# GpSimd makes the query-key products of a windowed attention, in halves of 1024 elements, and the schedule of the expert walk is paced for it

## The chip, the core and the metric

The kernel runs on one core of a Trainium2 chip. Its engines are called as in the profile: PE (TensorE, matrix products; PEld its weight loads), DVE (VectorE), ACT (ScalarE), POOL (GpSimd) and SP, which here only issues transfers. Each engine takes its own list of instructions in order and waits on semaphores for the others. The metric is the device time of one execution in microseconds (us).

## The reference

The input x is (2, 1024, 256) in float32. It is normalised over the last axis (xn), and the output is x plus an attention branch of xn plus a mixture-of-experts branch of xn.

The attention branch sees each batch as 64 × 64 × 4 = 16384 tokens of 16 channels. Two branches of 8 channels attend inside windows of 8 neighbouring tokens, one along rows and one along columns. Cut to what matters:

```python
qkv = (tok @ qkv_w).reshape(B, -1, 3, C)
attn = softmax(part(q) * scale @ swapaxes(part(k), -1, -2), axis=-1)
out = attn @ vw + lepe                       # lepe: a 3x3 depthwise convolution of v
att = concatenate([x1, x2], axis=-1) @ proj_w + proj_b
normed = (att - mu) * rsqrt(var + EPS) * ln_w + ln_b
return transpose(tok + normed, (0, 2, 1)).reshape(B, H, W)
```

The other branch routes each of the 2048 rows to 6 of 16 experts of 176 hidden units (silu(x Wg) * (x Wu), then Wd), weighted, and adds two shared experts.

## The kernel before

A prologue normalises x, computes the routing, sorts the rows by their sets of experts into 16 tiles of 128 rows, and does the shared experts. Then comes **the walk**, which this change concerns.

The walk goes over **slots**. A slot is one visit of one expert to one sorted tile: 16 tiles × 6 slots, and 26 slots called extras for tiles that need more experts, done after the first four tiles; 122 in all, and a loop for rare leftovers. Slots come in pairs (units) with a software pipeline over the unit u:

- `up` (L831 to L834), once a slot: PE multiplies the tile with the expert's gate and up weights into PSUM (pr_u, three buffers), ACT makes the silu (sg), and DVE multiplies sg, the routing weight and the up half into `hms`. There are two buffers of hms, each for one unit.
- `hidden` (L845, L847), once a unit, for unit u-1: PE transposes hms (ph), ACT copies it (hT).
- `finished`, once a unit, for unit u-2: PE multiplies with the down weights (pr_y, L857 for pairs, L865 for extras). DVE or ACT adds it to ysum (L912 for pairs, L920 for extras).
- `added`: when a tile's sum is complete, POOL scatters it into the output with an indirect DMA (L926). These accumulate into the same output, so each waits for the one before to land.

Between the slots the walk places the **steps of the attention**: after the preparation of weights, four blocks (batch b, head h), then eight steps `attended` (L750 on) that project, normalise and collect the attention's rows in `att`, and adds to the output (L954, POOL's queue).

A block has these steps. `project` (L660 to L665), eight times: PE makes q, k and v of an eighth of the block's tokens, ACT copies them into qk and v. Then four times, for 4 of 16 window groups (NW = 4): `products` (L673), DVE multiplies each query with each key element by element into a buffer of 2048 elements a partition, and `scores` (L677), DVE sums over the 8 channels. Then `highest` (L683 to L685): maximum, subtraction, and the exponential on ACT. Then four times `weighted` (L694) and `values` (L699), DVE's product of weights with values and its sum, and between them `totals` (L688, L689). Then `divide` (L707), and `transposed` (L714, L716): PE's transposes po and ACT's copy to oT. products and weighted use the same buffer (tag prod, one buffer).

The order of the work is decided twice. In the program, each step carries a pair of costs in us for DVE and PE, and a slot has such a pair too (`of_slot`). After every slot the walk emits steps as long as DVE's summed cost is no larger than `pace` times PE's:

```python
while step and done[0] <= pace * done[1]:
    step[2]()
    counted(step)
    last, step = step, next(walk, None)
    if last[1] > 1:
        break
```

`pace` is the ratio of the whole walk's DVE cost to its PE cost, both without the last END us of PE. Then the framework's scheduler orders the instructions of each engine by its own estimate of when they can start; the lists of the engines are fixed before the kernel runs.

Of the kernel before, what the change touches and what calls it, by code (L numbers as in the profile page):

```python
# [8 lines left out]
F32 = mybir.dt.float32  # L9
# [4 lines left out]
ALU = mybir.AluOpType  # L14
AX = mybir.AxisListType
# [7 lines left out]
P = 128  # L23
B, H, W = 2, 1024, 256
C = 16
HD = 8
WIN = 8
NW = 4
# [21 lines left out]
def csw_block_moe(ctx: ExitStack, tc: tile.TileContext, x, qkv_w, conv_w0, conv_b0, conv_w1, conv_b1,  # L50
# [19 lines left out]
    nc = tc.nc  # L70
# [3 lines left out]
    work = ctx.enter_context(tc.tile_pool(name="work", bufs=1))  # L74
# [8 lines left out]
    def by_hl(t):  # L83
        return t.rearrange("(p l) d -> p l d", l=16)
# [3 lines left out]
    for g in range(4):  # L88
        (nc.sync if g % 2 == 0 else nc.scalar).dma_start(out=xx[:, 4 * g : 4 * g + 4, 0:W],
                                                         in_=by_hl(x_rows)[:, 4 * g : 4 * g + 4, :])  # L90
# [41 lines left out]
    for b in range(B):  # L132
        nc.gpsimd.dma_start(out=lb[64 * b : 64 * b + 64, :],
                            in_=ln_b.rearrange("(c o) -> c o", o=1).unsqueeze(1).to_broadcast([C, 4, 1]))
# [14 lines left out]
    for c in range(16):  # L149
        n = sum(P // 2 if k % 2 == 0 else P for k in range(c)) + (((16 - c) * P - 1) / 2 if c % 2 == 0 else 0)  # L150
# [69 lines left out]
    def statistics(g):  # L220
        st = small.tile([P, 4, 6], F32, name="st")
        mv = small.tile([P, 4, 2], F32, name="mv")
        for l in range(4):
            nc.vector.bn_stats(out=st[:, l, :], in_=xx[:, 4 * g + l, 0:W])
        for l in range(4):
            nc.vector.bn_aggr(out=mv[:, l, :], in_=st[:, l, :])
        rs = small.tile([P, 4], F32, name="rs")
        nc.scalar.activation(rs, mv[:, :, 1], AF.Sqrt, bias=eps)
        return mv, rs
# [88 lines left out]
    held = statistics(0)  # L318
    for g in range(4):
        now, held = held, statistics(g + 1) if g < 3 else None  # L320
# [15 lines left out]
    full = [P, 16, E]  # L336
# [114 lines left out]
    for c in range(15, -1, -1):  # L451
        n = 16 - c
# [186 lines left out]

    oT = big.tile([P, 4, 2, 4, P], F32, name="oT", tag="oT")  # L640

    def attention(b, h):
        steps = []

        qk = work.tile([P, 2, 2, 8, WIN, HD], F32, tag="qk", name=f"qk{b}{h}")
        v = work.tile([P, 2, 8, HD, WIN], F32, tag="v", name=f"v{b}{h}")
        s = work.tile([P, 16, WIN, WIN], F32, tag="f1024", name=f"s{b}{h}", bufs=3)
        o = work.tile([P, 16, WIN, HD], F32, tag="f1024", name=f"o{b}{h}", bufs=3)
        sums = small.tile([P, 16, WIN], F32, name=f"sums{b}{h}", tag="sums")
        rows = work.tile([P, 8, P], F32, tag="f1024", name=f"rows{b}{h}", bufs=3)  # L650
        full = [P, NW, WIN, WIN, HD]

        def gather():
            for i in range(2):
                nc.scalar.copy(rows[:, 4 * i : 4 * i + 4].rearrange("p i (w r) -> p i w r", r=4),
                               xnT[:, h, :, 64 * b : 64 * b + 64].rearrange("p (i r) (w u) -> p u i w r", r=4, u=2)[:, i])

        def project(i):
            pq = ps_m.tile([P, 3, 8, C], F32, tag="m", name="pq")
            nc.tensor.matmul(pq.rearrange("p s t c -> p (s t c)"), lhsT=rows[:, i],  # L660
                             rhs=wq.rearrange("p s t c -> p (s t c)"), start=True, stop=True)
            nc.scalar.copy(qk[:, :, 0, i], pq[:, 0:2, :, 0:HD])  # L662
            nc.scalar.copy(qk[:, :, 1, :, i], pq[:, 0:2, :, HD:C])
            nc.scalar.copy(v[:, 0, i], pq[:, 2, :, 0:HD].rearrange("p t c -> p c t"))
            nc.scalar.copy(v[:, 1, :, :, i], pq[:, 2, :, HD:C])  # L665

        held = {}

        def products(n):
            pr = work.tile([P, NW, WIN, WIN, HD], F32, tag="prod", name="pr")  # L670
            br, m = n // 8, n % 8
            q_, k_ = (qk[:, part, br, m : m + NW] for part in range(2))
            nc.vector.tensor_tensor(pr, q_.unsqueeze(3).to_broadcast(full), k_.unsqueeze(2).to_broadcast(full), ALU.mult)  # L673
            held[n] = pr

        def scores(n):
            nc.vector.tensor_reduce(out=s[:, n : n + NW], in_=held.pop(n), axis=AX.X, op=ALU.add)  # L677

        rows_s = s.rearrange("p n q k -> p (n q) k")

        def highest():
            top = small.tile([P, P], F32, tag="top", name="top", bufs=1)
            nc.vector.tensor_reduce(out=top, in_=rows_s, axis=AX.X, op=ALU.max)  # L683
            nc.vector.tensor_tensor(rows_s, rows_s, top.unsqueeze(2).to_broadcast([P, P, WIN]), ALU.subtract)
            nc.scalar.activation(rows_s, rows_s, AF.Exp, scale=HD**-0.5)  # L685

        def totals():
            nc.vector.tensor_reduce(out=sums.rearrange("p n q -> p (n q)"), in_=rows_s, axis=AX.X, op=ALU.add)  # L688
            nc.vector.reciprocal(sums, sums)  # L689

        def weighted(n):
            pr = work.tile([P, NW, WIN, HD, WIN], F32, tag="prod", name="pv")
            br, m = n // 8, n % 8
            nc.vector.tensor_tensor(pr, s[:, n : n + NW].unsqueeze(3).to_broadcast(full),  # L694
                                    v[:, br, m : m + NW].unsqueeze(2).to_broadcast(full), ALU.mult)
            held[n] = pr

        def values(n):
            nc.vector.tensor_reduce(out=o[:, n : n + NW], in_=held.pop(n), axis=AX.X, op=ALU.add)  # L699

        def divide():
            xo = held["xo"] = work.tile([P, 8, 8, C], F32, tag="xo", name=f"xo{b}{h}")
            for br in range(2):
                to = xo[:, :, :, HD * br : HD * br + HD]
                if br:
                    to = to.rearrange("p i t c -> p t i c")
                nc.vector.tensor_tensor(to, o[:, 8 * br : 8 * br + 8],  # L707
                                        sums[:, 8 * br : 8 * br + 8, :].unsqueeze(3).to_broadcast([P, 8, WIN, HD]),
                                        ALU.mult)

        def transposed(i):
            po = ps_m.tile([P, 4, P], F32, tag="m", name="po")
            for j in range(4):
                nc.tensor.transpose(po[:, j, :], held["xo"][:, i + j].rearrange("p t c -> p (t c)"), ident)  # L714
            to = oT.rearrange("p g h r (b w i) -> p g h b i w r", b=B, i=2)[:, :, h, b, i // 4]
            nc.scalar.copy(to, po.rearrange("p j (w r) -> p j w r", r=4))  # L716


        steps.append((0.3, 0.0, gather))
        for i in range(8):  # L720
            steps.append((0.3, 0.65, lambda i=i: project(i)))
        for n in range(0, 16, NW):
            steps.append((2.3, 0.0, lambda n=n: products(n)))
            steps.append((2.3, 0.0, lambda n=n: scores(n)))
        steps.append((2.5, 0.0, highest))
        for n in range(0, 16, NW):
            steps.append((2.3, 0.0, lambda n=n: weighted(n)))
            if n == 0:
                steps.append((1.5, 0.0, totals))
            steps.append((2.3, 0.0, lambda n=n: values(n)))  # L730
        steps.append((1.4, 0.0, divide))
        for i in (0, 4):
            steps.append((0.3, 0.5, lambda i=i: transposed(i)))
        return steps
# [195 lines left out]
    att = []  # L930

    def all_steps():
        for steps in (extras_listed(), weights_prepared()):
            for _ in steps:
                yield 1.0, 0.1, lambda: None
        yield from attention_steps()

    def attention_steps():
        for b in range(B):
            for h in range(2):  # L940
                yield from attention(b, h)
        xe = []
        yield 0.6, 0.0, lambda: xe.extend(edges())
        att.extend(work.tile([P, 8, W], F32, tag=tag, name="att") for tag in ("prod", "qk"))
        for g in range(4):
            for h in range(2):
                yield 1.4, 3.9, lambda: attended(g, h, xe, att)
            if g % 2:
                waiting.extend([lambda m=m, b=b, n=g // 2: attention_added(m, b, n) for m in range(2) for b in range(B)])
# [7 lines left out]

    of_slot = {"six": (0.5, 2.0), "extra": (1.4, 2.25)}
    of_tile = (1.05, 0.25)
    END = 66  # L960
    in_walk = [11 * 1.0 + 4 * (16 * 2.3 + 3.3 + 2.5 + 1.5 + 1.4) + 0.6 + 8 * 1.4, 11 * 0.1 + 4 * 6.2 + 8 * 3.9]
    done = [0.0, 0.0]
    whole = [in_walk[n] + NTL * TOPK * of_slot["six"][n] + NX * of_slot["extra"][n] + NTL * of_tile[n] for n in range(2)]
    pace = (whole[0] - END * of_slot["six"][0] / of_slot["six"][1]) / (whole[1] - END)

# [121 lines left out]
```

## Time and profile before

| | |
|---|---|
| median of 7 runs (lowest to highest) | 466.79 us (464.4 to 470.0) |
| the profiled execution: time, span | 464.15 us, 462.4 us |
| granted TensorE clock, mean | 0.987 |
| PE, DVE, ACT, POOL busy | 412.6, 305.4, 214.2, 108.8 us |
| products L673 | 16 of 2289 ns, 36.6 us |
| scores L677 | 16 of 2280 ns, 36.5 us |
| weighted L694, values L699 | 16 of 2286 ns and 16 of 2268 ns |
| hms L834, pairs alone | 96 of 392 ns |
| scatters L926 on POOL | 16 of 1974 ns, 3.9 us to landing |

A timeline row of the profile has the start in us from the span's start, the duration in us, engine, line, operation, output and inputs, the shapes, how many instructions were merged into the row, and in brackets the idle time of the engine before it with what ended that. Rows of DVE overlap by some 0.08 us, so the distance from start to start is the better measure of what an instruction costs in a run of them. The chain of waits follows back from the last instruction what released it.

The walk runs in the profile from about 101 us (first slot) to 448 us. The four blocks' projections begin at 134.4, 196.3, 263.2 and 318.0 us, and the first attended step at 372.8 us.

### The profile page before, as it was taken

Reading aid. Unit: us, or ns where it says so; the run is one execution under the profiler, and the core shown is the slowest. Engines: PE = TensorE matmul, PEld = TensorE weight load, DVE = VectorE, ACT = ScalarE, POOL = GpSimd, SP = SyncE. Lnnn points to the kernel's source line nnn. Section 1 sums busy time; section 2 is a strip of 40 time slices with the busy share of each in tenths; the row PEclk is TensorE's granted clock in tenths of the full one; section 3 lists DMA queues with packets and bytes.
Section 4 is the critical chain, followed back from the end, with each engine's and each line's share of the span. In section 5 each row is a group of like instructions: output and inputs, shape, how many; then the busy total and the mean of one; then the engine's idle time right before and its main releaser. Section 6 shows DMA issues by size and latency. Waiting matters only on the chain.

```text
span 462.4 us, 6437 instructions
## 1 busy us (share of the span) xinstructions
PE 412.6 (89%) x1726; PEld 259.1 (56%) x1727; DVE 305.4 (66%) x555; ACT 214.2 (46%) x510; POOL 108.8 (24%) x127
## 2 busy tenths in 40 slices
PE   0999999996999998999999999998998889999980
PEld 0436566563666665655556666665666545556760
DVE  4525956745729999469999289995999932333220
ACT  2936167222354464463642453625343247778220
POOL 7300000426500000000001222110221126666821
PEclk9999999998999999999999999999999999999996
DMA  8999970423310010000001321201013110185552
GB/s 235 322 291 277 258 214 1 97 46 87 91 38 21 22 29 24 26 7 28 20 24 27 55 39 37 43 24 27 23 35 84 35 17 16 50 123 95 71 80 23
DMA packets 38323, 35.39 MB, mean 77 GB/s; under 512 B 4112, under 2 KB 36208, under 8 KB 38256
## 3 DMA queue, kind: packets, MB, share of 16 engines
q1 hardware_dynamic: 28336, 23.28, 18.3%
q0 software_dynamic: 8896, 10.65, 14.7%
q10 hardware_dynamic: 1056, 1.05, 0.7%
q8 instruction: 16, 0.26, 0.2%
q14 instruction: 19, 0.16, 0.1%
HBM read 26.44 MB, written 10.62 MB: 80 GB/s over the span
## 4 chain that ended last, share of the span: by engine, by line
PE 39%; DVE 35%; issue 9%; ACT 7%; DMA 6%; DVEq 1%; POOL 1%; POOLq 0%; SPq 0%; ACTq 0%
PE pr_u L831 10%; DVE pr L673 6%; PE pp L766 6%; DVE s L677 6%; DVE pv L694 5%; DVE o L699 5%; PE pr_y L857 5%; DVE hms L834 4%; PE pg L270 3%; DMA xg<-xw_d,of 3%; PE py L285 2%; PE pq L660 2%; PE pu L270 2%; DMA xx<-in_x_dram 2%; PE plT L252 2%
## 5 line engine op out<-in xcount | busy, mean ns | idle before, releaser
L831 PE MATMUL pr_u<-w1s,xsT 128*128 x384 | 127.8, 464 | 0.7 <-DVE hms L834 0.5
L833 ACT ACTIVATE sg<-pr_u 128x176 f32<-128x176 f32 x122 | 38.6, 318 | 134.5 <-PE pr_u L831 109.2
L831 PEld LDWEIGHTS pr_u<-w1s,xsT 128*128 128x128 f32 x384 | 71.6, 191 | 35.8 <-issue 5.5
L926 POOL DMA_INDIRECT out_dram<-ysum,of x16 | 31.6, 1974 | 225.2 <-ACT sg L833 124.5
L834 DVE SCALAR_TENSOR_TENSOR hms<-sg,w,pr_u 128x176 f32<-128x176 f32 x96 | 36.9, 392 | 35.3 <-ACT sg L833 35.3
L673 DVE TENSOR_TENSOR pr<-qk 128x2048 f32<-128x2048 f32 x16 | 36.6, 2289 | 20.0 <-ACT qk L662 19.7
L845 PE MATMUL ph<-ident,hms 128*128 128x128 f32 x183 | 33.8, 280 | 8.7 <-DVE hms L834 7.3
L845 PEld LDWEIGHTS ph<-ident,hms 128*128 128x128 f32 x183 | 23.4, 142 | 29.7 <-DVE hms L834 13.2
L694 DVE TENSOR_TENSOR pv<-s,v 128x2048 f32<-128x2048 f32 x16 | 36.6, 2286 | 2.4 <-ACT s L685 2.4
L677 DVE TENSOR_REDUCE s<-pr 128x256 f32<-128x2048 f32 x16 | 36.5, 2280 | 0.0
L699 DVE TENSOR_REDUCE o<-pv 128x256 f32<-128x2048 f32 x16 | 36.3, 2268 | 0.0
L831 PE MATMUL pr_u<-w1s,xd 128*128 x104 | 33.5, 460 | 0.0
L847 ACT COPY hT<-ph 128x384 f32<-128x384 f32 x61 | 29.1, 478 | 3.1 <-PE ph L845 1.5
L857 PE MATMUL pr_y<-w2a,hT 128*128 x96 | 28.7, 381 | 0.0
L857 PE MATMUL pr_y<-w2b,hT 112*128 x96 | 28.7, 379 | 0.0
L857 PE MATMUL pr_y<-wts,hT 128*128 128x256 f32 x96 | 28.6, 379 | 0.0
L660 PE MATMUL pq<-wq,rows 128*128 128x384 f32 x64 | 24.7, 502 | 2.8 <-ACT oT L716 2.1
L285 PE MATMUL py<-room 128*128 128x256 f32 x96 | 23.9, 387 | 1.5 <-DVE room L279 1.5
L831 PEld LDWEIGHTS pr_u<-w1s,xd 128*128 128x128 f32 x104 | 19.6, 190 | 9.3 <-issue 0.4
L270 PE MATMUL pg<-xnT,room 128*128 128x512 f32 x48 | 24.1, 614 | 0.0
L270 PE MATMUL pu<-xnT,room 128*128 128x512 f32 x48 | 23.0, 602 | 0.0
L285 PEld LDWEIGHTS py<-room 128*128 128x128 f32 x96 | 17.4, 190 | 6.8 <-DVE room L279 2.6
(320 smaller groups left out, 640.1 us busy)
## 6 DMA issues: line engine op xcount, KB each, us to landing
w1s<-in_w_dram SPq DMA_DIRECT2D x22, 256.0 KB, 5.5
wts<-in_w_dram SPq DMA_DIRECT2D x61, 64.0 KB, 2.1
wts<-in_w_dram SPq DMA_DIRECT2D x61, 48.0 KB, 1.8
xw_d<-xx SPq DMA_DIRECT2D x4, 544.0 KB, 8.9
w2a<-in_w_dram SPq DMA_DIRECT2D x4, 512.0 KB, 10.5
out_dram<-ysh POOLq DMA_DIRECT2D x4, 512.0 KB, 5.6
xr<-xw_d POOLq DMA_DIRECT2D x4, 512.0 KB, 5.0
out_dram<-att POOLq DMA_DIRECT2D x8, 256.0 KB, 6.7
```

Source lines behind the costliest of these rows:

```text
L270: nc.tensor.matmul(ps, lhsT=w1h[:, half, h, P * m : P * m + P], rhs=xnT[:, h, 4 * k : 4 * k + 4, :].rearrange("p l q -> p (l q)"), start=( ...
L285: nc.tensor.matmul(py, lhsT=hms[k, m][:, P * c : P * c + P], rhs=w2h[:, m], start=(m == 0), stop=(m == 2))
L660: nc.tensor.matmul(pq.rearrange("p s t c -> p (s t c)"), lhsT=rows[:, i], rhs=wq.rearrange("p s t c -> p (s t c)"), start=True, stop=True)
L673: nc.vector.tensor_tensor(pr, q_.unsqueeze(3).to_broadcast(full), k_.unsqueeze(2).to_broadcast(full), ALU.mult)
L677: nc.vector.tensor_reduce(out=s[:, n : n + NW], in_=held.pop(n), axis=AX.X, op=ALU.add)
L694: nc.vector.tensor_tensor(pr, s[:, n : n + NW].unsqueeze(3).to_broadcast(full), v[:, br, m : m + NW].unsqueeze(2).to_broadcast(full), ALU. ...
L699: nc.vector.tensor_reduce(out=o[:, n : n + NW], in_=held.pop(n), axis=AX.X, op=ALU.add)
L831: nc.tensor.matmul(pu, lhsT=lhs[:, h, :], rhs=w1s[:, :, h, bass.ds(e * I, I)], start=(h == 0), stop=(h == 1))
L833: nc.scalar.activation(sg, pu[:, 0, :], AF.Silu)
L834: nc.vector.scalar_tensor_tensor(hm[:, 0:I], sg, w, pu[:, 1, :], op0=ALU.mult, op1=ALU.mult)
L845: nc.tensor.transpose(ph[:, s, :], units[:, P * s : P * s + P], ident)
L857: nc.tensor.matmul(py, lhsT=l_, rhs=r_, start=start and n == 0, stop=stop and n == 2)
```

## The change

The products move from DVE to POOL (`nc.gpsimd.tensor_tensor`), in 8 chunks of 1024 elements a partition instead of 4 of 2048. One buffer `prods` of two halves is made once and kept for all blocks; the chunks alternate between the halves, and weighted uses both halves as one buffer of 2048. scores reduces a chunk of 1024 at a time. The steps are emitted one chunk apart (products of chunk n, then scores of chunk n-1), each with a DVE cost of 1.8 us instead of 2.3. The sum of costs `in_walk` and END (66 to 62) are changed to match, so `pace` becomes 1.33 instead of 1.18. The later buffer `att` takes the place of prods. In the changed file the lines are products L681, scores L685, maximum L691, weighted L702, values L707, hms L844, scatter L936.

```diff
+    prods_ = []
+
     def attention(b, h):
         steps = []
+        if not prods_:
+            prods_.append(work.tile([P, 2, NW // 2, WIN, WIN, HD], F32, tag="prod", name="prods"))
+        prods = prods_[0]
...
+        few = NW // 2
+        fewer = [P, few, WIN, WIN, HD]
+
         def products(n):
-            pr = work.tile([P, NW, WIN, WIN, HD], F32, tag="prod", name="pr")
+            pr = prods[:, n // few % 2]
             br, m = n // 8, n % 8
-            q_, k_ = (qk[:, part, br, m : m + NW] for part in range(2))
-            nc.vector.tensor_tensor(pr, q_.unsqueeze(3).to_broadcast(full), k_.unsqueeze(2).to_broadcast(full), ALU.mult)
+            q_, k_ = (qk[:, part, br, m : m + few] for part in range(2))
+            nc.gpsimd.tensor_tensor(pr, q_.unsqueeze(3).to_broadcast(fewer), k_.unsqueeze(2).to_broadcast(fewer), ALU.mult)
             held[n] = pr
 
         def scores(n):
-            nc.vector.tensor_reduce(out=s[:, n : n + NW], in_=held.pop(n), axis=AX.X, op=ALU.add)
+            nc.vector.tensor_reduce(out=s[:, n : n + few], in_=held.pop(n), axis=AX.X, op=ALU.add)
...
         def weighted(n):
-            pr = work.tile([P, NW, WIN, HD, WIN], F32, tag="prod", name="pv")
+            pr = prods.rearrange("p a w q k d -> p (a w) q k d")
...
-        for n in range(0, 16, NW):
-            steps.append((2.3, 0.0, lambda n=n: products(n)))
-            steps.append((2.3, 0.0, lambda n=n: scores(n)))
+        for n in range(0, 16 + few, few):
+            if n < 16:
+                steps.append((1.8, 0.0, lambda n=n: products(n)))
+            if n >= few:
+                steps.append((1.8, 0.0, lambda n=n: scores(n - few)))
...
-    END = 66
-    in_walk = [11 * 1.0 + 4 * (16 * 2.3 + 3.3 + 2.5 + 1.5 + 1.4) + 0.6 + 8 * 1.4, 11 * 0.1 + 4 * 6.2 + 8 * 3.9]
+    END = 62
+    in_walk = [11 * 1.0 + 4 * (16 * 1.8 + 8 * 2.3 + 3.3 + 2.5 + 1.5 + 1.4) + 0.6 + 8 * 1.4, 11 * 0.1 + 4 * 6.2 + 8 * 3.9]
```

More of the change, by code (lines that the diff above doesn't have):

```diff
@@ L943, in attention_steps @@
         yield 0.6, 0.0, lambda: xe.extend(edges())
-        att.extend(work.tile([P, 8, W], F32, tag=tag, name="att") for tag in ("prod", "qk"))
+        att.extend([prods_[0].rearrange("p a w q k d -> p (a w q k d)").rearrange("p (n d) -> p n d", d=W),
+                                       work.tile([P, 8, W], F32, tag="qk", name="att")])
         for g in range(4):
```

## The prediction, made before the changed kernel was run

> **What bounds the kernel now.** I read the page first: busy shares, slices, the chain.
>
> ```profile
> PE 412.6 (89%) x1726; PEld 259.1 (56%) x1727; DVE 305.4 (66%) x555; ACT 214.2 (46%) x510; POOL 108.8 (24%) x127
> ...
> DVE  4525956745729999469999289995999932333220
> ...
> POOL 7300000426500000000001222110221126666821
> ...
> PE 39%; DVE 35%; issue 9%; ACT 7%; DMA 6%; DVEq 1%; POOL 1%; POOLq 0%; SPq 0%; ACTq 0%
> ```
>
> PE (TensorE) is busy nearly everywhere, so a gain needs PE's waits to go. DVE (VectorE) is at nine tenths in four stretches, the four attention blocks (two batches, two heads), where POOL (GpSimd) is nearly idle. The chain runs through DVE there: L673, L677, L694, L699. Next, the timeline of DVE and of PE in the fourth block:
>
> ```profile
> 322.01 2.29 DVE L673 TENSOR_TENSOR pr<-qk 128x2048 f32<-128x2048 f32 x1 [5.57 <-ACT qk L662]
> 324.22 0.39 DVE L834 SCALAR_TENSOR_TENSOR hms<-sg,w,pr_u 128x176 f32<-128x176 f32 x1
> 324.53 2.28 DVE L677 TENSOR_REDUCE s<-pr 128x256 f32<-128x2048 f32 x1
> ...
> 342.59 1.22 DVE L683 TENSOR_REDUCE top<-s 128x128 f32<-128x1024 f32 x1
> ...
> 346.39 2.29 DVE L694 TENSOR_TENSOR pv<-s,v 128x2048 f32<-128x2048 f32 x1 [0.81 <-ACT s L685]
> ...
> 370.83 0.41 DVE L912 TENSOR_TENSOR ysum<-ysum,pr_y 128x256 f32<-128x256 f32 x1
> ```
>
> ```profile
> 317.99 1.81 PE L660 MATMUL pq<-wq,rows 128*128 128x384 f32 x4 [0.70 <-ACT oT L716]
> ...
> 336.49 2.53 PE L831 MATMUL pr_u<-w1s,xsT 128*128 x8
> 338.85 0.27 PE L845 MATMUL ph<-ident,hms 128*128 128x128 f32 x1
> 339.92 0.44 PE L845 MATMUL ph<-ident,hms 128*128 128x128 f32 x2 [0.80 <-DVE hms L834]
> ...
> 372.77 1.12 PE L766 MATMUL pp<-xnT,lp 128*128 128x512 f32 x2
> ```
>
> A block is a DVE chain: projection at 317.99, first product 4.0 later, products and scores to 342.6 (20.6), maximum to weights 3.8, values 24.4 to 370.8; the next PE stage starts 1.9 later. It lasts 54.8 us. Beside it PE does 20 to 22 slots of expert work. A slot has one hms on DVE; two slots are a unit of 4.0 us on PE (transposes L845 at 436.52 and 440.52 in the chain). PE waits for hms, 0.3 to 0.9 us at a time: it can run only two slots ahead, since the transposes (ph) after slot 2u+2 need the hms of slot 2u. All of PE's waits for DVE in the walk, by the waits view, are 7.3 (hms), 3.4 (ysum) and 1.7 (xo): 12.4 us. That is the largest gain that a lighter DVE could give.
>
> **What the change removes and adds.** DVE loses 16 products of 2.29 = 36.6 us. The 16 reductions of 2048 become 32 of 1024; the nearest row is the maximum over 1024 (L683, 1.22, its successor starting after 1.13): 32 × 1.2 = 38.4 against 36.5. DVE's net relief is some 35 us. POOL gets 32 products. Its nearest rows:
>
> ```profile
> 381.51 1.27 POOL L782 TENSOR_TENSOR a<-a,lw 128x512 f32<-128x512 f32 x1 [7.45 <-DVE a L781]
> 382.87 2.09 POOL L787 TENSOR_TENSOR att<-a,xr 128x256 f32<-128x256 f32 x2
> ```
>
> Two halves of 1.27 less one start (0.1, the smallest memset) make 2.44 for 1024 elements. Low end: the line through 256 elements in 1.05 and 512 in 1.27 gives 1.72. High end: four of L787's 1.05 are 4.2; that row reads with long strides, the products read runs of 8 contiguous floats with a broadcast, like L782's runs of 16. So I take 2.45 with the gap to the next.
>
> [...]
>
> What matters is that a chunk on POOL (2.45) costs as much as half a product and half a score on DVE (2.28): the chain through a score phase, 8 × 2.45 + 1.2 for the last reduction = 20.8, is no shorter than the 20.6 of now. POOL can't start early: prods is the buffer of the values too, and qk comes from PE and ACT. Two halves let POOL run back to back.
>
> **What the order does.** The built program lists each engine's instructions. DVE's list for the third block from the first product or score to the maximum (P product, S score, h hms, y ysum, T maximum):
>
> ```
> before  P h S P h S h P h S h y P h S h T
> after   S h S S S S S h S h S T
> ```
>
> Each S now waits for POOL, and the hms behind it wait with it. PE gets three hms in 20 us where it got seven, so it runs dry: the up products (L831) of two slots ahead, then nothing. The values phase has its products and reductions as before, with one hms after nearly each, so PE doesn't catch up there either. The rest of the slots, whose hms stand after the block's last DVE step (X), must still pass on PE before the next block's transposes and projections, which PE's list has at the same slots as before or one to three later. In the third block X comes after hms 76 (before: 80), and PE's transposes po after slot 83: at X PE has just transposed slots 77 and 78, and 1.3 + 2 × 4.0 + 1.2 + po 1.0 + copy 0.7, less 0.9 already gone, make 11.3 us until the next projection, with DVE and POOL idle. Before, that step took 3.1 (third) and 1.9 us (fourth).
>
> **The sum by blocks**, from projection to projection (the fourth to the first pp at L766):
>
> - Third, 54.8 now. POOL's list has five scatters (L926 of before) ahead of its products. They start 1.2 after the last L920 of the extras and lasted 251.41 to 272.29; so the first product starts 7.4 after the projection, not 1.9. 7.4 + 20.8 + 3.8 + 24.4 + 11.3 = 67.7: +12.9.
> - Fourth, 54.8. 1.9 + 20.8 + one scatter in the middle of POOL's list 1.6 + 3.8 + 24.4 + 11.3 = 63.8: +9.0.
> - Second, 66.9 (it carries the extras). 1.9 + 20.8 + maximum to X 32.5 (222.9 to 254.5 now, and its ysum wait behind S too) + 19.6 from X to the projection (nine slots of 2.0, po and copy 1.7) = 74.8: +7.9.
> - First: the projection comes after slot 8, not 12, about 125.0 instead of 134.4. Then 1.9 + 20.8 + one gather 1.0 + 3.8 + 24.4 = 51.9, X at 177; from there nine slots, four of them extras at 2.2, and po and copy, 21.8 in all, to the second projection at 198.7 against 196.32: +2.4.
>
> Together +32.2 at the first pp. The tail: from the first pp to the end are 89.6 us, carried by POOL (eight attended steps until 433.2, then four adds to the output, whose landing at 444.3 lets the last scatters go at 4.6 each). Attended starts some two slots nearer the end of PE's work, which would give back 3 us only if PE carried the tail. POOL's new list puts one scatter between those adds, and it waits for the first add to land. Before: 4.7 of issue, 6.4 of wait, two scatter rounds of 4.65, 20.4 in all; after: a landing of 6.7, a round of 4.65, three issues 3.5, 6.4, a round of 4.65, 25.9: up to +5.5. I take +1.3, midway between -3 and that. Sum +33.5: the execution of 464.15 becomes 497.7. The median of the runs is 466.79, 2.6 above that execution; with it 500.
>
> What is priced at nothing: END and the new pace only move steps among slots, which the lists already contain; SP's list keeps its loads in the same order and number, and no DMA is added. DVE's relief of 35 us is worth nothing here, because DVE stands waiting for POOL in the score phases and for PE between the blocks. If the hms were spread among the S, it would be worth up to the 12.4.
>
> On the read side: in the trace POOL's L782 took 1.27 beside DVE work and 1.94 and 1.87 twice, when its own DMA issue was still running (403 to 408, 415 to 417); no row shows a DVE product against it. [...]
>
> **Rivals.** (1) POOL's chunk is short, and the change gains. Every 0.1 us of the chunk is 3.2 us (32 chunks in the chain), so the loss is gone at about 1.4, and below that PE's waits go too: at best 466.8 − 12.4 = 454. For it: POOL's 256 to 512 elements cost only 0.22. Against: 512 already take 1.27. At the line's 1.72 it is still 476. Chance of faster 0.05, of no change 0.03 (0.5%, 2.3 us, is what a measurement can tell). (2) The chunk costs as L787 does, 4.2: 56 more, 556; against it the contiguous runs; 0.06. (3) PE keeps more in hand than two slots, so that only the chain counts: the third and fourth block then end as now, 3.1 and 1.9 after X instead of 11.3, which is 18 less, 482, and a little less still in the second; against it the ph waits above; 0.12. The rest, 0.74, is the sum, 485 to 515.
>
> **How the numbers follow.** 500 is the likeliest. The low end 480 takes in most of rival 3 and a chunk of 1.8; the high end 522 a chunk of 3.0 with the whole tail. Slower by over 0.5% 0.92.
>
> **What would show it.** POOL's products near 2.4 us, back to back, 32 of them; DVE idle before the S, released by POOL, some 8 to 12 us a block; PE's ph waiting for hms several us at a time in the score phases; X to projection about 11 us in the third block; the first product of the third block behind the scatters; DVE's busy time near 270. Wrong: POOL chunks under 1.5, PE busy through the score phases, or a span under 475.

## The result, and the profile after

The changed kernel takes 497.19 us (median of 18 runs, 495.54 to 499.48) against 467.05 us (46 runs, 464.25 to 472.65): a ratio of 1.064, with a 95% interval of 1.0618 to 1.0661. It is slower by 30.1 us. Its profiled execution took 497.47 us, with a span of 495.8 us against 462.4 and a mean granted TensorE clock of 0.958 against 0.987.

The page of the kernel after: busy times, slices of DVE, of POOL and of the granted clock, and the chain by engine.

```profile
PE 422.2 (85%) x1726; PEld 264.0 (53%) x1727; DVE 278.6 (56%) x555; ACT 213.8 (43%) x510; POOL 178.3 (36%) x159
...
DVE  5518776745578953269982158962589713333200
POOL 7200001256681000590003692114921323776531
PEclk9999999999998999997999988999989999999975
...
PE 36%; DVE 23%; POOL 13%; DMA 12%; issue 9%; ACT 6%; DVEq 0%; POOLq 0%; SPq 0%; ACTq 0%
```

DVE shed 26.8 us, POOL took on 69.5, and neither brought time. PE's idle time (span less busy) rose from 49.8 to 73.6 us, and the same 1726 matmuls are busy for 9.6 us more: 23.8 + 9.6 = 33.4, the whole growth of the span. The chain now runs through POOL for 13% of the span, from 1%.

The groups of the products and of their sums (total busy, mean ns, then idle time before them and its releaser):

```profile
L681 POOL TENSOR_TENSOR prods<-qk 128x1024 f32<-128x1024 f32 x32 | 75.2, 2520 | 68.9 <-ACT qk L667 67.6
...
L685 DVE TENSOR_REDUCE s<-prods 128x128 f32<-128x1024 f32 x32 | 39.0, 1219 | 48.0 <-POOL prods L681 48.0
```

DVE stands 48 us in front of the sums, waiting for POOL: 12 us a block. Busy time over 32 gives 2.35 us a chunk; the median of one is 2354 ns too.

DVE's timeline in the third block, from before its first sum to its last, and the block's X (xo):

```profile
274.89 0.40 DVE L844 SCALAR_TENSOR_TENSOR hms<-sg,w,pr_u 128x176 f32<-128x176 f32 x1 [1.11 <-ACT sg L843]
282.92 1.22 DVE L685 TENSOR_REDUCE s<-prods 128x128 f32<-128x1024 f32 x1 [7.63 <-POOL prods L681]
284.06 0.39 DVE L844 SCALAR_TENSOR_TENSOR hms<-sg,w,pr_u 128x176 f32<-128x176 f32 x1
285.23 1.22 DVE L685 TENSOR_REDUCE s<-prods 128x128 f32<-128x1024 f32 x1 [0.78 <-POOL prods L681]
...
294.40 1.22 DVE L685 TENSOR_REDUCE s<-prods 128x128 f32<-128x1024 f32 x1 [1.07 <-POOL prods L681]
295.54 0.39 DVE L844 SCALAR_TENSOR_TENSOR hms<-sg,w,pr_u 128x176 f32<-128x176 f32 x1
...
327.04 1.28 DVE L715 TENSOR_TENSOR xo<-o,sums 128x512 f32<-128x512 f32 x2
```

Between the hms at 284.06 and the one at 295.54 stand five sums, 2.3 us apart, each waiting for a chunk. DVE is idle for nearly half of that stretch (5.1 of 11.5 us), and yet it can't take the next hms. PE's timeline over the same time:

```profile
288.73 1.35 PE L841 MATMUL pr_u<-w1s,xsT 128*128 x4
295.98 2.71 PE L841 MATMUL pr_u<-w1s,xsT 128*128 x4 [5.91 <-DVE hms L844]
...
299.13 1.06 PE L867 MATMUL pr_y<-w2a,hT 128*128 x2
...
339.66 1.81 PE L665 MATMUL pq<-wq,rows 128*128 128x384 f32 x4 [0.69 <-ACT oT L724]
```

PE does the up product ahead, then waits 5.91 us for the hms behind the sums. At the end of the block DVE has done X at 328.3, but PE, late with its slots, starts the next projection only at 339.66, 11.3 us later.

All times of a block can be read from four marks of the timelines: its first projection, its maximum, the end of X (of the last xo), and the next block's projection (for the fourth block the first pp). Summed over the four blocks:

| kernel | projection to maximum | maximum to X | X to next stage | first projection at | first pp at | first pp to end |
|---|---|---|---|---|---|---|
| before | 98.9 | 117.0 | 22.6 | 134.4 | 372.8 | 89.7 |
| after | 94.6 | 116.8 | 64.6 | 127.2 | 403.2 | 92.6 |

The chain through the scores is not what got longer; it is 4.3 us shorter in all. The loss of 42.0 us is all between X and the next stage, where DVE and POOL are done with the block and PE still has slots of expert work ahead of the next stage. With −4.3 and −0.2 from the other two columns, 7.2 given back by the earlier start of the first block, and 2.9 more in the tail, that is 33.2, the 33.4 of the spans but for rounding.

### The profile page after: what moved, and what is told of

Same layout as the page of the kernel before. It is cut to its first block, busy times and chain, and to the rows that moved or that the text cites. A ratio compares the mean times of both kernels' runs of the same rounds, so it can differ in the third digit from the quotient of the medians.

```text
span 495.8 us, 6479 instructions
## 1 busy us (share of the span) xinstructions
PE 422.2 (85%) x1726; PEld 264.0 (53%) x1727; DVE 278.6 (56%) x555; ACT 213.8 (43%) x510; POOL 178.3 (36%) x159
## 4 chain that ended last, share of the span: by engine, by line
PE 36%; DVE 23%; POOL 13%; DMA 12%; issue 9%; ACT 6%; DVEq 0%; POOLq 0%; SPq 0%; ACTq 0%
POOL prods L681 10%; PE pr_u L841 9%; PE pp L776 6%; DVE prods L702 5%; DVE o L707 5%; DMA out_dram<-ysum,of 5%; PE pr_y L867 4%; DMA xg<-xw_d,of 3%; PE pr_y L875 3%; PE pg L270 2%; DVE hms L844 2%; PE py L285 2%; PE pu L270 2%; DMA xx<-in_x_dram 2%; PE plT L252 2%
## 5 line engine op out<-in xcount | busy, mean ns | idle before, releaser
L841 PE MATMUL pr_u<-w1s,xsT 128*128 x384 | 131.3, 473 | 16.2 <-DVE hms L844 15.8
L841 PEld LDWEIGHTS pr_u<-w1s,xsT 128*128 128x128 f32 x384 | 71.8, 193 | 53.4 <-DVE hms L844 19.9
L681 POOL TENSOR_TENSOR prods<-qk 128x1024 f32<-128x1024 f32 x32 | 75.2, 2520 | 68.9 <-ACT qk L667 67.6
L936 POOL DMA_INDIRECT out_dram<-ysum,of x16 | 27.1, 1695 | 120.2 <-DVE ysum L922 55.7
L685 DVE TENSOR_REDUCE s<-prods 128x128 f32<-128x1024 f32 x32 | 39.0, 1219 | 48.0 <-POOL prods L681 48.0
L844 DVE SCALAR_TENSOR_TENSOR hms<-sg,w,pr_u 128x176 f32<-128x176 f32 x96 | 37.0, 391 | 50.2 <-ACT sg L843 50.2
L855 PE MATMUL ph<-ident,hms 128*128 128x128 f32 x183 | 34.6, 286 | 6.4 <-DVE hms L844 5.8
L702 DVE TENSOR_TENSOR prods<-s,v 128x2048 f32<-128x2048 f32 x16 | 36.6, 2287 | 2.1 <-ACT s L693 2.1
L707 DVE TENSOR_REDUCE o<-prods 128x256 f32<-128x2048 f32 x16 | 36.4, 2276 | 0.0
L841 PE MATMUL pr_u<-w1s,xd 128*128 x104 | 34.9, 477 | 0.0
L867 PE MATMUL pr_y<-w2a,hT 128*128 x96 | 30.1, 396 | 0.0
L288 POOL DMA_DIRECT2D out_dram<-ysh x4 | 3.7, 922 | 64.6 <-ACT ysh L286 64.6
L841 PEld LDWEIGHTS pr_u<-w1s,xd 128*128 128x128 f32 x104 | 20.6, 199 | 10.1 <-issue 1.6
L812 POOL DMA_INDIRECT xg<-xw_d,of x16 | 16.3, 1017 | 19.1 <-PE px__929 L816 9.3
```

The costliest lines, as they stand in the source:

```text
L681: nc.gpsimd.tensor_tensor(pr, q_.unsqueeze(3).to_broadcast(fewer), k_.unsqueeze(2).to_broadcast(fewer), ALU.mult)
L685: nc.vector.tensor_reduce(out=s[:, n : n + few], in_=held.pop(n), axis=AX.X, op=ALU.add)
L841: nc.tensor.matmul(pu, lhsT=lhs[:, h, :], rhs=w1s[:, :, h, bass.ds(e * I, I)], start=(h == 0), stop=(h == 1))
L844: nc.vector.scalar_tensor_tensor(hm[:, 0:I], sg, w, pu[:, 1, :], op0=ALU.mult, op1=ALU.mult)
L855: nc.tensor.transpose(ph[:, s, :], units[:, P * s : P * s + P], ident)
L867: nc.tensor.matmul(py, lhsT=l_, rhs=r_, start=start and n == 0, stop=stop and n == 2)
```

## Experiments

**The theory:** hms, queued behind sums that wait for POOL, starve PE; the next block's stage then waits for PE's slots. **The rivals:** the new pacing by itself; POOL's rate, whatever the order; the chunks and the shared room. The ratio is always to runs of the kernel before on the same chip, with its 95% interval.

**e1_pace_only.** The kernel before with the new pacing:

```diff
-            steps.append((2.3, 0.0, lambda n=n: products(n)))
-            steps.append((2.3, 0.0, lambda n=n: scores(n)))
+            steps.append((3.6, 0.0, lambda n=n: products(n)))
+            steps.append((3.6, 0.0, lambda n=n: scores(n)))
...
-    END = 66
+    END = 62
...
```

The sum of costs `in_walk` is changed to match, as in the kernel after.

> The kernel before, VectorE still making the products 2048 at a time, but with the walk paced as in the kernel after (each of these steps counted at 3.6, the sum for the walk and END as after). Theory (the scores' sums wait for GpSimd's chunks with the gated units hms queued behind them): no such wait exists here, and the list has the attention steps at nearly the same slots as before, so 465 to 474 us. Rival (the pacing, not the move, spreads the attention badly): most of the 30 us, 485 us or more.

Measured: 468.03 us, ratio 1.0016 (0.9990 to 1.0042). Pacing alone costs nothing that can be told; X to the next stage is 31.5.

**e2_move_only.** The kernel after with before's pacing:

```diff
-                steps.append((1.8, 0.0, lambda n=n: products(n)))
+                steps.append((1.15, 0.0, lambda n=n: products(n)))
...
-                steps.append((1.8, 0.0, lambda n=n: scores(n - few)))
+                steps.append((1.15, 0.0, lambda n=n: scores(n - few)))
...
-    END = 62
+    END = 66
...
```

`in_walk` is that of before too.

> The kernel after, GpSimd making the products in chunks, but paced by the numbers of before. Theory: the chunks' chain of 2.3 us a chunk and the sums ahead of the hms are still there, so 488 to 502 us. Rival (pacing): 465 to 475 us.

Measured: 490.32 us, ratio 1.0527 (1.0449 to 1.0604); X to the next stage 50.6. The move alone makes most of the loss. The pacing, harmless before, adds to it here.

**e7_dve_chunks.** Chunks, room and pacing of after, with VectorE making the products:

```diff
-            nc.gpsimd.tensor_tensor(pr, q_.unsqueeze(3).to_broadcast(fewer), k_.unsqueeze(2).to_broadcast(fewer), ALU.mult)
+            nc.vector.tensor_tensor(pr, q_.unsqueeze(3).to_broadcast(fewer), k_.unsqueeze(2).to_broadcast(fewer), ALU.mult)
```

> The kernel after with its chunks, its shared room and its pacing, but VectorE making the products. Theory (the sums' wait for the other engine puts hms behind it): chunk product and sum together keep VectorE 2.4 us a chunk and nothing waits for GpSimd, so X to the next projection is as with the pacing alone (2 to 14 us) and the time 466 to 474 us. Rival (the halves of one room, or 32 short steps for 16 long ones, cost the time): 485 us or more.

Measured: 470.24 us, ratio 1.0055 (1.0023 to 1.0086). Chunks and room cost little; making the products on POOL, with the list that comes of it, makes the other 27 us. X to the next stage is 37.3; 16.0 of it is the first block's, above the 2 to 14 expected, and the other three lie within. That is far from the 64.6 of the kernel after.

**e3_half_product.** The chunk at half its length, the other half of its products left out:

```diff
+            nc.vector.memset(prods_[0], 0.0)
...
-            nc.gpsimd.tensor_tensor(pr, q_.unsqueeze(3).to_broadcast(fewer), k_.unsqueeze(2).to_broadcast(fewer), ALU.mult)
+            half = [P, few, WIN, WIN // 2, HD]
+            nc.gpsimd.tensor_tensor(pr[:, :, :, 0 : WIN // 2], q_.unsqueeze(3).to_broadcast(half),
+                                    k_[:, :, 0 : WIN // 2].unsqueeze(2).to_broadcast(half), ALU.mult)
```

> The kernel after with GpSimd multiplying only half of the keys of each chunk (512 elements); the other half of the products is a zero written once, so half of the score products are left out. Theory: the blocks hang on GpSimd's chain of chunks; at half the elements a chunk takes 1.2 to 1.4 us, the score phase falls from 20.8 to 11 us, bound then by the sums' 1.22 us, and four blocks give back 25 to 38 us: 460 to 472 us. Rival (the loss lies in where the steps stand, whatever a chunk takes): 485 us or more.

Measured: 475.25 us, ratio 1.0179 (1.0110 to 1.0249), above the range that was expected. The chunk's median fell from 2354 to 1273 ns, 34.6 us over 32 of them; projection to maximum fell by 24.8, less than that, as POOL now waits for qk between some chunks (0.46 to 0.60 us each in the fourth block), and X to the next stage stayed, 66.2 after 64.6. With a chunk as short as the sum itself the kernel still loses to before: a shorter chunk shortens the chain but doesn't bring hms forward in the list.

**e4_in_order.** The kernel after, with one rule for DVE's list:

```diff
+    last_hms = []
...
-        nc.vector.scalar_tensor_tensor(hm[:, 0:I], sg, w, pu[:, 1, :], op0=ALU.mult, op1=ALU.mult)
+        last_hms[:] = [nc.vector.scalar_tensor_tensor(hm[:, 0:I], sg, w, pu[:, 1, :], op0=ALU.mult, op1=ALU.mult).ins]
...
-                step[2]()
+                with tc.issue_after(last_hms[0]):
+                    step[2]()
```

The rule fixes only the place in the list: what a step puts on DVE goes behind the hms written last; it waits for nothing more. It binds every step of the attention, not the sums alone.

> The kernel after with the order of VectorE's list alone changed: each attention step of VectorE is queued behind the hms that the walk wrote before it, so that hms stand among the sums as they are written and not behind a row of them. Theory (PE starves because hms stand behind sums that wait for GpSimd): the chain of a block stays at 20 us for the scores but PE works through it; most of the loss goes, 468 to 482 us. Rival (GpSimd's rate by itself, or slower matmuls, make the loss): no gain, 490 to 500 us.

Measured: 468.59 us, ratio 1.0051 (1.0021 to 1.0080): 28.6 of the 30.1 us are gone. DVE's timeline in the third block of this kernel:

```profile
274.67 1.22 DVE L685 TENSOR_REDUCE s<-prods 128x128 f32<-128x1024 f32 x1 [1.09 <-POOL prods L681]
275.80 0.39 DVE L846 SCALAR_TENSOR_TENSOR hms<-sg,w,pr_u 128x176 f32<-128x176 f32 x1
276.97 1.22 DVE L685 TENSOR_REDUCE s<-prods 128x128 f32<-128x1024 f32 x1 [0.78 <-POOL prods L681]
278.11 0.39 DVE L846 SCALAR_TENSOR_TENSOR hms<-sg,w,pr_u 128x176 f32<-128x176 f32 x1
279.27 1.22 DVE L685 TENSOR_REDUCE s<-prods 128x128 f32<-128x1024 f32 x1 [0.77 <-POOL prods L681]
280.40 0.39 DVE L846 SCALAR_TENSOR_TENSOR hms<-sg,w,pr_u 128x176 f32<-128x176 f32 x1
```

The sums still come every 2.3 us and still wait for POOL, but an hms stands in each gap. The waits of PE in the kernel after, then in this one (total, times, longest):

```profile
PE pr_u L841 <- DVE hms L844: 15.8, 6, 5.9
...
PE ph L855 <- DVE hms L844: 5.8, 9, 0.9
```

```profile
PE ph L857 <- DVE hms L846: 6.5, 11, 0.9
...
PE pr_u L843 <- DVE hms L846: 1.6, 3, 0.8
```

Projection to maximum grew from 94.6 to 125.7 us, most of it in the first two blocks, where the sums now stand behind hms and ysum that wait for ACT and PE; X to the next stage fell from 64.6 to 7.9. The slower chain is the faster kernel.

**e10_half_in_order.** The edits of e3_half_product and e4_in_order together.

> The kernel with the order rule (e4_in_order) and GpSimd multiplying only half of the keys of each chunk, the other half of the products being a zero written once; half of the score products are left out. It tells whether a chunk's time still counts when the order is right. Theory: PE is no longer starved there, so halving a chunk brings little: 460 to 468 us. Rival (GpSimd's rate bounds the blocks in either order): 440 to 456 us.

Measured: 469.65 us, ratio 1.0052 (1.0029 to 1.0076), like e4_in_order with the whole chunk, though 1.7 us above the range expected. Out of order, half a chunk brought 22 us; in order it brings nothing. With the list in order, POOL's rate is no bound at these lengths.

**e8_before_order** and **e9_order_paced** put the same rule into the kernel before, and into e2_move_only: one list rule, one pacing, two engines (e9_order_paced keeps the chunks and the shared room as well).

> The kernel before with the same ordering rule and nothing else changed, to price the rule by itself. Theory: its VectorE list already alternates attention steps and hms, so the rule changes little: 463 to 469 us. Rival (the rule is worth most of the 29 us that it gave the kernel after, whatever engine makes the products): 455 us or less.

> The kernel after with the ordering rule and the pacing of before: against e8_before_order (rule and pacing the same, VectorE making the products) it prices the move alone once hms are no longer behind the sums. Theory: the chain of a block is no shorter than with VectorE making the products (8 chunks of 2.3 and a sum are 19.6 against 18.3 of products and sums without hms), so no gain: 463 to 470 us. Rival (VectorE's 35 us of relief pay once the order is right): 452 to 460 us.

Measured: e8_before_order 463.87 us, ratio 0.9910 (0.9872 to 0.9949), the only version here that beats both kernels; e9_order_paced 467.39 us, ratio 1.0002 (0.9966 to 1.0038). The rule is worth 4.5 us where DVE makes the products and 23 where POOL does (490.32 to 467.39). With the list in order, the move, with its chunks and room, still costs some 0.9%, and DVE's relief shows nowhere. X to the next stage is 8.3 in both, and projection to maximum 104.1 and 104.6.

**e6_alternate** and **e6_alternate_o** share the work: POOL makes every second chunk, DVE the others, with the scheduler's order and with the rule.

```diff
-            nc.gpsimd.tensor_tensor(pr, q_.unsqueeze(3).to_broadcast(fewer), k_.unsqueeze(2).to_broadcast(fewer), ALU.mult)
+            (nc.gpsimd if n // few % 2 else nc.vector).tensor_tensor(pr, q_.unsqueeze(3).to_broadcast(fewer), k_.unsqueeze(2).to_broadcast(fewer), ALU.mult)
...
+        for n in range(0, 16, NW):
+            steps.append((0.0, 0.0, lambda n=n: products(n + few)))
+            for at in (n, n + few):
+                if at == n:
+                    steps.append((1.2, 0.0, lambda at=at: products(at)))
+                steps.append((1.2, 0.0, lambda at=at: scores(at)))
...
```

END is 66 and `in_walk` counts these steps; e6_alternate_o has the rule of e4_in_order besides.

> Shared work: GpSimd makes every second chunk of 1024 into the second half of the room while VectorE makes and sums the other, paced by the steps' own sizes (1.2 each); the scheduler orders VectorE's list. From the traces, two chunks keep VectorE 1.2 + 1.22 + 1.22 = 3.6 us in place of 4.57, and GpSimd's 2.3 to 2.5 us lie beside the first two, so a block's score phase is 3 to 4 us shorter than before. Theory: if no long row of sums is put ahead of hms, 456 to 466 us; if the scheduler puts SSP ahead of hms as in the list of the first block, some of it is lost, up to 475. Rival (any product on GpSimd costs): above 475 us.

> The same shared work, with each attention step of VectorE queued behind the hms written before it. Theory: as e6_alternate but without sums ahead of hms; X to the next projection near 2 us as in the run with the order alone, score phases 3 to 4 us shorter per block than before, 455 to 464 us. Rival (TensorE is the bound by now, what VectorE saves is not seen): 464 to 469 us.

Measured: 479.72 us, ratio 1.0238 (1.0185 to 1.0291), and 472.10 us, ratio 1.0071 (1.0035 to 1.0106). Both expectations missed, the first into its rival's range, the second above both of its ranges: a score phase is not 3 to 4 us shorter. Two timelines of e6_alternate_o, DVE's products (L681) and POOL's, tell why:

```profile
279.82 1.22 DVE L681 TENSOR_TENSOR prods<-qk 128x1024 f32<-128x1024 f32 x1
...
284.75 3.25 DVE L681 TENSOR_TENSOR prods<-qk 128x1024 f32<-128x1024 f32 x1
```

```profile
280.05 3.19 POOL L681 TENSOR_TENSOR prods<-qk 128x1024 f32<-128x1024 f32 x1 [1.40 <-DVE s L685]
284.58 2.34 POOL L681 TENSOR_TENSOR prods<-qk 128x1024 f32<-128x1024 f32 x1 [1.33 <-DVE s L685]
```

Where DVE's product starts 0.23 us ahead, POOL's takes 3.19 us instead of 2.34; where POOL's starts 0.17 ahead, DVE's takes 3.25 instead of 1.22. Each ends about when it would if it began after the other's end. Of the 16 chunks on POOL six took 3.19 to 3.26 so and one 2.91, and of the 16 products on DVE five took 3.25 to 3.34 and one 1.58. Sums and hms beside a chunk kept their 1.22 and 0.39. So a pair of chunks takes DVE 4.6 to 4.9 us from product to product where it is shortest, up to 7.9 elsewhere with other work between, and never less than the 4.57 of a product and a sum of 2048 on DVE alone. A third room, with which POOL's chunk could lie beside the sums only, was not tried.

## Why the prediction was right

The forecast was 500.0 in a range of 480 to 522, with slower at 0.92; measured were 497.2. By its own steps:

- **The order as the mechanism** is shown: the list alone, changed in e4_in_order, takes 28.6 of the 30.1 us away. Why the scheduler sets the sums ahead of the hms was not looked into. The wait shows one instruction earlier than named: PE's long waits are at the up product L841, which needs a PSUM buffer that an hms frees, while ph waits 0.9 at most.
- **X to the next projection**, forecast 11.3 for the third and fourth block, measured 11.3 and 11.3. The 3.1 given for the third block before is 2.2 in the trace (X ends at 315.83, the projection begins at 317.99); the sum doesn't use it.
- **The blocks:** second 74.8 forecast and measured; fourth 63.8 and 63.5; third 67.7 and 63.6. The third's miss is the scatters' rounds:

```profile
262.08 1.64 POOL L936 DMA_INDIRECT out_dram<-ysum,of  x1 [40.05 <-DVE ysum L930]
266.16 1.57 POOL L936 DMA_INDIRECT out_dram<-ysum,of  x1 [2.44 <-DMA out_dram<-ysum,of]
...
278.97 1.54 POOL L936 DMA_INDIRECT out_dram<-ysum,of  x1 [2.99 <-ACT v L670]
279.96 7.54 POOL L681 TENSOR_TENSOR prods<-qk 128x1024 f32<-128x1024 f32 x3
```

  They were 4.1 to 4.5 us apart, not the 4.5 to 5.5 of before, and the third projection came 2.6 later than forecast, so the products began 3.9 after it and not 7.4.
- **The first block** began at 127.2 (forecast 125.0) and took 74.1 (73.7). The sum has no term for DVE and POOL holding each other up, and this trace shows one case: the preparation of a sorted tile puts a small DVE copy among the sums:

```profile
143.29 3.16 DVE L819 COPY wsrt<-xg 128x16 f32<-128x16 f32 x1
```

```profile
139.47 6.94 POOL L681 TENSOR_TENSOR prods<-qk 128x1024 f32<-128x1024 f32 x3
147.65 2.34 POOL L681 TENSOR_TENSOR prods<-qk 128x1024 f32<-128x1024 f32 x1 [1.24 <-DVE s L685]
```

  The copy, 0.17 to 0.18 in most of the sixteen tiles, ends with POOL's third chunk of this row, at 146.4. It holds DVE 3.0 us longer; POOL's last chunk, which needs the half that a sum behind the copy frees, starts 1.24 late. So it is 1.2 us on the block's chain, priced at nothing.
- **The chunk** was priced at 2.45 with its gap; sums come 2.30 apart. Eight chunks and the last sum took 20.3 in the third block, not 20.8.
- **The tail** was priced +1.3 by a scatter between the adds, and grew by 2.9. e1_pace_only and e7_dve_chunks, with no chunk on POOL, have 91.8 and 92.0, so at least part of it doesn't come from POOL; its causes aren't separated.
- **The sum** of +33.5 meets the +33.4 of the spans. That it is this close is luck: the first block's later start (+2.2), its length (+0.4) and the tail (+1.6) happen to cancel the third block (−4.1) and the fourth (−0.3). Of the 2.8 us by which 500.0 is too high, 2.6 is the distance of before's profiled execution to its median; after's execution lay at its median.
- **Rival 1** had its break-even at a chunk of 1.4 us. That was wrong: at 1.27 the kernel still loses 1.8%. 3.2 us for each 0.1 supposes that nothing but POOL sets the chain; the runs give 22 us for 1.08, 2.0 for each 0.1.
- **Rival 3**, PE with more slots in hand, falls with the 5.91 us wait. The bound of 12.4 for DVE's relief with hms spread among the sums was too generous: in order, the move brings nothing (e9_order_paced against e8_before_order).
- **DVE's busy time** was put near 270 and is 278.6: the copy above is 3.0 of it.

## What to carry to other kernels

When an operation moves to another engine, read the list of the engine that keeps its consumer: the consumer becomes a wait in an in-order queue, and what stands behind it pays, even if both engines have time to spare (here the order of one list was 28.6 of the 30.1 us). Fix the place of the short instruction that feeds the bounding engine first; only then does the moved operation's own rate matter, and here it did not. Time two engines' products side by side before sharing work between them: here one of two that met took up to 3.34 us instead of 1.22, or 3.26 instead of 2.34.

## What the runs showed of the hardware that was not expected

PE's matmuls were slower for a while after some of its waits. After the idle 5.91 us the next four up matmuls took 2.71 us, not the 1.35 to 1.45 of others, and the next pair of pr_y 1.06, not 0.60; at 300.75 they are back. The windows view gives the granted clock over the 27 us from the third projection, ahead of the share of DMA and GB/s: first the kernel after, then e4_in_order.

```profile
276.00:303.00 27.00, 20.96 (x70) 13.50 (x71) 13.43 (x15) 10.57 (x44) 19.99 (x9) 0.87 0.13 21
```

```profile
265.00:292.00 27.00, 26.89 (x105) 17.81 (x104) 13.42 (x20) 12.34 (x50) 21.77 (x11) 1.00 0.20 34
```

In the same time PE did 70 matmuls at a clock of 0.87, against 105 at 1.00. From 113 to 450 us the granted clock is 1.00 in the kernel before (in e4_in_order 1.00 from 265 to 319 us), and 0.97 in the kernel after, which has four stretches at half clock there, one a block (the other two are 222.14 to 228.97 and 365.50 to 368.91):

```profile
150.46:153.87 3.41, 3.09 (x10) 1.97 (x9) 3.38 (x5) 0.58 (x1) 0.00 (x0) 0.50 0.00 0
...
293.82:300.65 6.83, 4.67 (x11) 3.27 (x12) 4.68 (x6) 1.90 (x4) 5.13 (x3) 0.50 0.00 0
```

PE is busy for 17.4 us in the four. By the doubled time of the up matmuls above, half of that, some 8.7 us, is an estimate of what they add, and so of most of the 9.6 us of added busy time; in e4_in_order PE is busy for 413.4 us, against 412.6 before. No term of the sum has it. In the third block it cost the chain nothing that shows: at 316.5 PE waits for an hms again (1.58 us), so it had caught up with DVE before X.

What brings these stretches on isn't shown. In the third and fourth block PE waited for 5.91 and 4.72 us about their start; in the first two its waits just before were 1.96 and 1.89 us. Of the 3.41 us ahead of each, as long as the shortest of them, PE was busy for 1.45, 1.21, 0.00 and 0.40 us, in the order of the blocks.

Two products, one on DVE and one on POOL, did not run side by side: 3.25 and 3.19 us above, against the 1.22 and 2.34 of others. A DVE copy of 16 elements that met chunks took 3.16, against 0.17 to 0.18 in most tiles, while sums and hms beside chunks kept 1.22 and 0.39. What in these instructions decides it no row tells.
